# Order of p*v and projection, and the form of the range folds, in the first cross-attention of a Perceiver kernel on Trainium2

## Chip, core and metric

The kernel runs on one core of a Trainium2 chip, in fp32. The metric is the device time of one launch in microseconds (us). Three runs of the kernel before took 1648.14, 1651.96 and 1657.2 us, so the median is 1651.96 us.

## What is computed

128 tokens of 256 features pass through six blocks: a cross-attention to 12544 context rows of 192 features, a causal self-attention, a mixture of eight experts, a second cross-attention, a second self-attention, a second mixture. The change lies in the first block alone:

```python
q = (x @ Wq + bq).reshape(B, N, NUM_HEADS, HEAD_DIM)       # x layer-normed, 16 heads of 16
k = (y @ Wk + bk).reshape(B, M, NUM_HEADS, HEAD_DIM)       # y: the 12544 context rows
v = (y @ Wv + bv).reshape(B, M, NUM_HEADS, HEAD_DIM)
attn = jax.nn.softmax(jnp.einsum('bnhd,bmhd->bhnm', q, k) * scale, axis=-1)
out = jnp.einsum('bhnm,bmhd->bnhd', attn, v).reshape(B, N, IMAGE_DIM)
h = jax.nn.relu(out @ W1 + b1)
return h @ W2 + b2
```

## The kernel before

**Tiling.** The 16 heads are taken as two octets. For each octet the context is walked in 13 superblocks: twelve of 1024 keys, and a short one of 256. A superblock is cut into groups of 256 keys, so an octet has 49 groups and the stage has 98, numbered t = 0 to 97. `groups[t]` is a pair (m, g): superblock and group in it. A group's scores are 2 x 1024 columns on 128 partitions, in two tiles k = 0 and 1.

**Ranges.** The softmax's maximum is not taken over all keys at once. Groups are gathered into ranges of ten, and the fifth range of each octet has nine: ranges b = 0 to 9, where b = 4 and b = 9 are the short ones. A running maximum `mx[b]` is kept during the range. At the range's end `fold(b)` (L442) takes the maximum over the two 256-column halves, `range_maximum` (L455, L456) turns the result on TensorE and reduces it to `negmax`, and one step later (two steps for b = 4) `range_spread` (L255) and `range_spread_out` (L476) write the shift back in the scores' layout, into `spreads[b]`.

**Pipeline.** A step t of the main loop works on several groups at once. TensorE's order is written out by hand:

- `scores(t)` (L411), then `range_spread` where it is due;
- the projection `pieces(t + 4)`: at g = 0 both 64-row parts and the first half of the keys (L214, L217), at g = 1 the second half of the keys, at g = 2 and 3 the same for the values (L232, L239). A short superblock does all four at once;
- `attend(t - 13)`, p*v (L512);
- `range_maximum`, if the range ended with the step before.

`same` in the main loop exchanges projection and p*v: where the superblock that is projected and the one that is attended use the same of the five value tiles (`m % NV`), p*v goes first. For the plain part of the stage that is one step in four, the one with g = 0. In steps 45 to 61, where the short superblock has moved the phase, it is every step.

**The other engines in a step.** ScalarE copies the scores out of PSUM (L424) and takes the exponents of group t - 12 (L499). VectorE takes the running maximum (L430), the fold if one is due, one share of the shift (L488, one SBUF and one PSUM input), and evicts the projections (L372 keys, L376 values, which are queued behind the fold). GpSimd does the larger share of the shift (L488, two SBUF inputs); its instructions for a whole range need only `spreads[b]` and scores kept long ago, so it runs through them without a stop.

**Buffers.** Scores have two PSUM tiles of two banks. Projections and transposes share the two banks of tag "w" (`ps_w`). One bank "m" holds a shift that VectorE still reads. For the two nine-group ranges it is not free when the maximum is due, and both transposes then use "w". A range's probabilities lie in a ring of 28 SBUF tiles (`slot`), which also takes the weights of later blocks. `mx` has one buffer, `spreads` two.

Of the kernel before, what the change touches and what calls it, by code (L numbers as in the profile page):

```python
# [8 lines left out]
F32 = mybir.dt.float32  # L9
AF = mybir.ActivationFunctionType  # L10
ALU = mybir.AluOpType
AX = mybir.AxisListType

P = 128
# [19 lines left out]
def perceiver(ctx: ExitStack, tc: tile.TileContext, a: dict, out: bass.AP):  # L34
    nc = tc.nc
# [17 lines left out]
    def ps_w(name):  # L53
        return banks["pool"].tile([P, KB], F32, tag="w", name=name, bufs=banks["w"])

    def slot(name):

        return ring.tile([P, 2 * KB], F32, tag="p", name=name)
# [32 lines left out]
    ident = const.tile([P, P], F32, name="ident")  # L91
# [97 lines left out]
    NS = (SK + SB - 1) // SB  # L189
# [114 lines left out]
    with tc.tile_pool(name="l0w", bufs=1) as lw:  # L304
# [4 lines left out]
        with psum_pool("ps0", 2) as pp, tc.tile_pool(name="l0x", bufs=1) as work:  # L309
# [3 lines left out]
            AHEAD, LAG = 4, 13  # L313
            NV = 5
            sbs = [(j, s) for j in range(2) for s in range(NS)]
            groups = [(m, g) for m, (j, s) in enumerate(sbs) for g in range(min(SB, SK - s * SB) // 256)]
# [3 lines left out]
            range_of, start_of = [], []  # L320
# [4 lines left out]
            last_of = [t for t in range(len(groups)) if last[t]]  # L325

            kTs, ps, mx, spreads, kept, os, deferred = {}, {}, {}, {}, {}, {}, {}
# [3 lines left out]
            NR = len(start_of)  # L331
# [12 lines left out]
            for j in range(2):  # L344
                pq = ps_mm(f"x0_pq{j}")
                for c in range(2):
                    nc.tensor.matmul(
                        pq[:, :P], xwq[:, c, j * P : (j + 1) * P], xnT[:, c, :], start=(c == 0), stop=(c == 1)
                    )
                qT = work.tile([P, P], F32, tag="qT", name=f"x0_qT{j}", bufs=2)  # L350
                nc.vector.tensor_scalar(
                    qT, pq[:, :P], cols[:, COL_BQ + j : COL_BQ + j + 1], 0.25, ALU.add, ALU.mult
                )
                for u in range(2):
                    nc.vector.tensor_scalar(qz[:, j, u, :], qT, parity[:, u : u + 1], None, ALU.mult)
# [81 lines left out]

            def fold(b):

                for k in (1, 0):  # L440
                    m = mx[b][:, k].rearrange("p a (c n) -> p a c n", c=2)
                    nc.vector.tensor_tensor(m[:, :, 0], m[:, :, 0], m[:, :, 1], ALU.max)  # L442

            def bank_m(name):
                return pp.tile([P, KB], F32, tag="m", name=name, bufs=1)

            def range_maximum(b):
                for k in (1, 0):

                    free = last_of[b] + 1 - LAG + 2 >= start_of[b] - 1  # L450
                    pt = bank_m(f"x0_mt{b}_1") if k and free else ps_w(f"x0_mt{b}_{k}")
                    for a in range(2):
                        for u in range(2):
                            n0 = (2 * a + u) * P
                            nc.tensor.transpose(pt[:, n0 : n0 + P], mx[b][:, k, a, u * P : (u + 1) * P], ident)  # L455
                    nc.vector.tensor_reduce(  # L456
                        negmax[:, b].rearrange("p (u i) -> p i u", u=2)[:, 2 * k : 2 * k + 2],
                        pt.rearrange("p (a u q) -> p a u q", a=2, u=2), AX.X, ALU.max, negate=True,
                    )
# [10 lines left out]
                return pbs  # L470

            def range_spread_out(b, pbs):
                spreads[b] = work.tile([P, 3, 256], F32, tag="spread", name=f"x0_spread{b}", bufs=2)
                for k in range(2):
                    n = 2 - k
                    nc.scalar.copy(spreads[b][:, 2 * k : 2 * k + n], pbs[k][:, :n])  # L476
# [13 lines left out]
            def shifted_gpsimd(t):  # L490
                for k in range(2):
                    shift(nc.gpsimd, t, k, slice(0, shares(t)[k]), spreads[range_of[t]][:, 2 * k :])
# [40 lines left out]
            with tc.manual_schedule():  # L533
                for t in range(AHEAD):
                    for f in pieces(t):
                        f()
                oTs = {}

                spread_at = {max(l + 2, l0 + LAG - 2): b for b, (l0, l) in enumerate(zip(start_of, last_of))}
                for t in range(len(groups) + LAG + 1):  # L540
                    e, o = t - LAG + 1, t - LAG
                    e = e if 0 <= e < len(groups) else None
                    o = o if 0 <= o < len(groups) else None
                    st = scores(t) if t < len(groups) else None
                    ended = range_of[t - 1] if 1 <= t < len(groups) + 1 and last[t - 1] else None
                    b = spread_at.get(t)
                    spread = range_spread(b) if b is not None else None
                    if e is not None:
                        shifted_gpsimd(e)
                        if first[e]:  # L550
                            shifted_vector(e)
                    if t < len(groups):
                        keep(t, st)
                    if spread:
                        range_spread_out(b, spread)
                    if e is not None:
                        for k in range(2):
                            exponent(e, k)
                    if ended is not None:
                        fold(ended)  # L560
                    if 0 <= t - LAG + 2 < len(groups) and not first[t - LAG + 2]:
                        shifted_vector(t - LAG + 2)
                    ahead = pieces(t + AHEAD)

                    same = o is not None and ahead and groups[t + AHEAD][0] % NV == groups[o][0] % NV
                    for f in () if same else ahead:
                        f()
                    if o is not None:
                        attend(o)
                        if last[o]:  # L570
                            oTs[range_of[o]] = collected(range_of[o])
                    for f in ahead if same else ():
                        f()
                    if ended is not None:
                        range_maximum(ended)
                    if t > LAG and last[t - LAG - 1]:
                        g = range_of[t - LAG - 1]
                        gather(g, oTs.pop(g))

                nr = NR // 2  # L580
                acc = work.tile([P, 2, 8, 17], F32, name="x0_acc")
                allneg = small.tile([P, 2, 8], F32, tag="allneg", name="x0_allneg")
                by_octet = negmax.rearrange("p (j b) h -> p j b h", j=2)
                nc.vector.tensor_reduce(allneg, by_octet.rearrange("p j b h -> p j h b"), AX.X, ALU.min)
                fall = work.tile([P, 2, nr, 8], F32, name="x0_fall")
                nc.vector.tensor_tensor(
                    fall, allneg.unsqueeze(2).to_broadcast([P, 2, nr, 8]), by_octet, ALU.subtract
                )
                nc.scalar.activation(fall, fall, AF.Exp)
                nc.vector.tensor_tensor(  # L590
                    accs, accs, fall.rearrange("p j b h -> p (j b) h").unsqueeze(3).to_broadcast([P, NR, 8, 17]),
                    ALU.mult,
                )
                for j in range(2):
                    nc.vector.tensor_reduce(
                        acc[:, j].rearrange("p h d -> p (h d)"),
                        accs[:, j * nr : (j + 1) * nr].rearrange("p b h d -> p (h d) b"), AX.X, ALU.add,
                    )
# [13 lines left out]
            o = slot("x0_o")[:, :D]  # L612
# [23 lines left out]
        with tc.tile_pool(name="l0a", bufs=1) as work:  # L636
# [3 lines left out]
            for j in range(4):  # L640
# [5 lines left out]
                b = cols[:, COL_AQK + j : COL_AQK + j + 1]  # L646
                if j < 2:
                    qT = work.tile([P, P], F32, tag="qT", name=f"a0_qT{j}", bufs=2)
# [11 lines left out]
            acc = work.tile([P, NH, 17], F32, name="a0_acc")  # L660
            for g in range(2):
# [9 lines left out]
                p = work.tile([P, 8, P], F32, tag="ap", name=f"a0_p{g}", bufs=2)  # L671
# [10 lines left out]
            o = normalised(work, acc, 16, "a0_o")  # L682
# [50 lines left out]
    with tc.tile_pool(name="l1x", bufs=1) as work:  # L733
# [6 lines left out]
        ctxs, kTs, vs, ps, mx, sums, spreads, os = {}, {}, {}, {}, {}, {}, {}, {}  # L740
# [4 lines left out]
        qT = work.tile([P, 8, P], F32, name="x1_qT")  # L745
        for g in range(2):
            pq = ps_mm(f"x1_pq{g}")
            for i in range(4):
                j = 4 * g + i
# [185 lines left out]
        with tc.manual_schedule():  # L935
# [7 lines left out]
            for t in range(NP + LAG):  # L943
# [3 lines left out]
                o = attend(before) if 0 <= before else None  # L947
# [4 lines left out]
                k = keys(t + 1) if t + 1 < NP else None  # L952
# [25 lines left out]
                short = k and v and periods[t + 1][1] == NS - 1  # L978
# [180 lines left out]
```

## Time and profile before

| what | value |
|---|---|
| median of three runs | 1651.96 us (1648.14 to 1657.2) |
| the profiled execution's own time | 1656.36 us |
| its span, first to last instruction | 1654.3 us |
| first attention, loop steps 0 to 97 (first scores to the last fold) | 22.0 to 460.7 us |
| GpSimd's first shift of range 0 and of range 8 | 69.50 and 427.51 us |

Busy times are read per engine, and an engine's idle time counts only where it is the one that the others wait for. A line of the timeline gives start, duration, engine, source line, operation, output and inputs with shapes, the number of instructions merged, and in brackets the idle time before it with what ended it. A line of the window table gives, for one stretch, the busy time and instruction count of PE (TensorE's matmuls), PEld (its weight loads), DVE (VectorE), ACT (ScalarE) and POOL (GpSimd), then the share of full clock granted to TensorE and the DMA load.

### The profile page before, as it was taken

The page shows a single profiled execution, that of the slowest core. Times are in us where ns is not written, and L with a number is a line of the kernel's source. Part 1 is how long each engine was busy: PE and PEld are TensorE (multiplying, and loading weights), DVE is VectorE, ACT ScalarE, POOL GpSimd, SP SyncE. Part 2 cuts the span into 40 slices and gives each one's busy share as a digit, 9 for nine tenths or more (in the row PEclk, how much of TensorE's full clock was granted, in tenths as well). Part 3 has the DMA queues.
Part 4 walks back from the last instruction along what each step waited for, and adds up shares of the span by engine and source line. Part 5 has one row for each costly group of instructions (what it writes and reads, how often), then busy time and mean ns, then how long its engine had stood idle before and what let it go on. Part 6 is the DMA issues. An engine that isn't in the chain of part 4 may idle for free.

```text
span 1654.3 us, 39758 instructions
## 1 busy us (share of the span) xinstructions
PE 1540.8 (93%) x17143; PEld 1177.7 (71%) x17143; DVE 1188.2 (72%) x1267; ACT 979.5 (59%) x1178; POOL 857.6 (52%) x554
## 2 busy tenths in 40 slices
PE   7899988999867988999999999999999999999978
PEld 4566655666545874688778777788777777787868
DVE  5788887888874214577777787777777777778952
ACT  2688878889871113466566556566565655665531
POOL 1378777878730000086476575665764864862000
PEclk9999999999986989999999999999999999999979
DMA  3111011111083326423222222332322322234940
GB/s 100 39 59 40 26 59 40 53 46 40 13 272 111 102 52 171 120 79 96 82 78 82 88 87 63 97 90 73 94 78 83 92 82 82 78 97 135 295 141 4
DMA packets 68421, 145.58 MB, mean 88 GB/s; under 512 B 8851, under 2 KB 27027, under 8 KB 68246
## 3 DMA queue, kind: packets, MB, share of 16 engines
q1 hardware_dynamic: 68246, 143.04, 28.9%
q8 instruction: 135, 2.21, 0.6%
q14 instruction: 40, 0.33, 0.1%
HBM read 142.87 MB, written 0.13 MB: 86 GB/s over the span
## 4 chain that ended last, share of the span: by engine, by line
PE 76%; DVE 13%; ACT 8%; issue 2%; DMA 1%; POOLq 0%; ACTq 0%; DVEq 0%; SPq 0%
PE x_k L217 13%; PE x_v L239 11%; PE x_s L808 11%; PE x_o L882 10%; PE x_v L232 6%; PE x_k L214 6%; PE x_s L411 4%; DVE x_mx L430 3%; ACT x_p L424 3%; ACT x_p L499 3%; PE x_o L512 3%; PE f_h L716 2%; PE f_h L1095 2%; PE f_py L726 2%; DVE x_part L905 1%
## 5 line engine op out<-in xcount | busy, mean ns | idle before, releaser
L863 POOL TENSOR_TENSOR x_p<-x_p,x_spread 128x1024 f32<-128x1024 f32 (+1 forms) x175 | 402.8, 2326 | 201.2 <-ACT x_spread L856 201.1
L488 POOL TENSOR_TENSOR x_p<-x_p,x_spread 128x512 f32<-128x512 f32 (+1 forms) x184 | 325.6, 1816 | 142.6 <-ACT x_spread L476 70.1
L905 DVE TENSOR_REDUCE x_part<-x_p 128x256 f32<-128x1024 f32 (+1 forms) x175 | 329.2, 1921 | 1.3 <-ACT x_p L871 1.3
L832 DVE TENSOR_TENSOR x_mx<-x_s,x_mx 128x1024 f32<-128x1024 f32 (+1 forms) x184 | 221.0, 1201 | 148.0 <-PE x_s L808 137.2
L825 ACT COPY x_p<-x_s 128x1024 f32<-128x1024 f32 (+1 forms) x200 | 199.2, 996 | 187.4 <-DVE x_mx L832 108.7
L910 POOL TENSOR_TENSOR x_sums<-x_sums,x_part 128x256 f32<-128x256 f32 x161 | 121.1, 752 | 303.2 <-DVE x_part L905 303.0
L424 ACT COPY x_p<-x_s 128x1024 f32<-128x1024 f32 x196 | 193.4, 1015 | 93.2 <-PE x_s L411 78.6
L239 PEld LDWEIGHTS x_v<-ywv_lo,x_ctx_lo 128*128 128x128 f32 x1568 | 189.3, 192 | 38.3 <-issue 36.8
L808 PE MATMUL x_s<-x_qT,x_kT 64*128 64x128 f32 x3136 | 203.0, 279 | 3.9 <-ACT x_p L825 3.9
L808 PEld LDWEIGHTS x_s<-x_qT,x_kT 64*128 64x128 f32 x3136 | 183.1, 188 | 28.2 <-issue 15.6
L871 ACT ACTIVATE x_p<-x_p 128x1024 f32<-128x1024 f32 (+1 forms) x200 | 197.8, 1037 | 1.4 <-DVE x_p L863 1.3
L499 ACT ACTIVATE x_p<-x_p 128x1024 f32<-128x1024 f32 x196 | 196.3, 1062 | 0.4 <-DVE x_p L488 0.4
L217 PE MATMUL x_k<-x_ctx_lo,ywk_lo 128*128 128x512 f32 (+1 forms) x412 | 194.2, 594 | 0.0
L882 PE MATMUL x_o<-x_p,x_v 128*64 128x128 f32 x3136 | 193.6, 276 | 0.4
L239 PE MATMUL x_v<-ywv_lo,x_ctx_lo 128*128 128x128 f32 x1568 | 193.1, 276 | 0.0
L430 DVE TENSOR_TENSOR x_mx<-x_s,x_mx 128x1024 f32<-128x1024 f32 x140 | 168.1, 1221 | 31.6 <-PE x_s L411 16.8
L882 PEld LDWEIGHTS x_o<-x_p,x_v 128*64 128x64 f32 x3136 | 169.6, 137 | 12.3 <-issue 1.5
L793 ACT COPY x_v<-x_v 128x512 f32<-128x512 f32 (+1 forms) x208 | 116.4, 562 | 76.4 <-PE x_v L239 75.7
L232 PEld LDWEIGHTS x_v<-ywv_hi,x_ctx_hi 64*128 64x128 f32 x1568 | 107.3, 189 | 49.3 <-issue 25.0
L779 ACT COPY x_kT<-x_k 128x512 f32<-128x512 f32 (+1 forms) x104 | 58.3, 561 | 138.2 <-PE x_k L217 138.2
L512 PE MATMUL x_o<-x_p,x_v 128*32 128x128 f32 x3136 | 122.0, 279 | 18.9 <-ACT x_p L499 18.0
L411 PE MATMUL x_s<-x_qz,x_kT 32*128 32x256 f32 x1568 | 119.0, 403 | 15.9 <-ACT x_p L424 15.6
(242 smaller groups left out, 1729.8 us busy)
## 6 DMA issues: line engine op xcount, KB each, us to landing
x_ctx_lo<-in_ctxT_dram SPq DMA_DIRECT2D x131, 512.0 KB, 4.1
x_ctx_hi<-in_ctxT_dram SPq DMA_DIRECT2D x262, 128.0 KB, 4.0
f_w<-in_L_ffn_W_dram SPq DMA_DIRECT2D x32, 512.0 KB, 6.6
f_gating<-n_kernel_gating_EDF_dram SPq DMA_DIRECT2D x8, 512.0 KB, 7.0
f_up<-L_ffn_kernel_up_EDF_dram SPq DMA_DIRECT2D x8, 512.0 KB, 7.3
f_wd<-ffn_kernel_down_EFD_dram SPq DMA_DIRECT2D x8, 512.0 KB, 7.0
x_ctx_lo<-in_ctxT_dram SPq DMA_DIRECT2D x11, 128.0 KB, 2.1
xw<-in_L_xattn_W_dram SPq DMA_DIRECT2D x2, 512.0 KB, 4.8
```

Of the source, the lines that this page charges most:

```text
L217: nc.tensor.matmul(ps[r][:, :h], wk[0][:, js], lo[:, r * h : (r + 1) * h], start=False, stop=True)
L232: nc.tensor.matmul(ps[r][:, ks], hi[rs, ks], wv[1][rs, js], start=(kc == 0), stop=False, skip_group_check=True,)
L239: nc.tensor.matmul(ps[r][:, kc * P : (kc + 1) * P], lo[:, r * h + kc * P : r * h + (kc + 1) * P], wv[0][:, js], start=False, stop=True, sk ...
L424: nc.scalar.copy(ps[t][k], st[k].rearrange("p a n -> p (a n)"))
L430: nc.vector.tensor_tensor(m, st[1 - k], old, ALU.max)
L488: engine.tensor_tensor(v, v, by[:, banks].unsqueeze(2).to_broadcast([P, n, 2, 256]), ALU.add)
L499: nc.scalar.activation(ps[t][k], ps[t][k], AF.Exp)
L808: nc.tensor.matmul(st[:, u, c * P : (c + 1) * P], kTs[t][rs, ks], qT[rs, j, :], start=True, stop=True)
L832: nc.vector.tensor_tensor(mx[j][:, :, : n * P], sts[i], old, ALU.max)
L863: engine.tensor_tensor(v, v, spreads[j].unsqueeze(2).to_broadcast([P, 2, n, P]), ALU.add)
L882: nc.tensor.matmul(o[us, 0:P], vs[t][:, c0 + c, us], p[:, n0 : n0 + P], start=(c0 + c == 0), stop=(c0 + c == total - 1), skip_group_check= ...
L905: nc.vector.tensor_reduce(part, v, AX.X, ALU.add)
```

## The change

1. `same`, the condition under which p*v goes ahead of the projection, is narrowed from "same value tile" to "same tile, and the projection writes the part that p*v reads". It now holds at t = 44, 48, 52, 56, 60 and 93 and no longer at the 27 other steps of 33 (16, 20, ..., 40; 45 to 47; 49 to 51; 53 to 55; 57 to 59; 61, 65, ..., 89).
2. `fold` writes into the tile `spreads[b]` instead of in place, for all ranges. For b = 4 and 9 it is a `tensor_reduce` over pairs (one input) instead of a `tensor_tensor` (two inputs). The transposes of `range_maximum` read `spreads[b]`.
3. `spreads[b]` becomes 4 x 256 instead of 3 x 256 and is taken at the fold. To make room, `qT` has one buffer instead of two, and `x0_acc` and `x0_fall` move into the ring.

```diff
             def fold(b):
+                spreads[b] = work.tile([P, 4, 256], F32, tag="spread", name=f"x0_spread{b}", bufs=2)
                 for k in (1, 0):
-                    m = mx[b][:, k].rearrange("p a (c n) -> p a c n", c=2)
-                    nc.vector.tensor_tensor(m[:, :, 0], m[:, :, 0], m[:, :, 1], ALU.max)
+                    dst, m = spreads[b][:, 2 * k : 2 * k + 2], mx[b][:, k].rearrange("p a (c n) -> p a c n", c=2)
+                    if last_of[b] - start_of[b] < 9:
+                        nc.vector.tensor_reduce(dst, m.rearrange("p a c n -> p a n c"), AX.X, ALU.max)
+                    else:
+                        nc.vector.tensor_tensor(dst, m[:, :, 0], m[:, :, 1], ALU.max)
...
-                            nc.tensor.transpose(pt[:, n0 : n0 + P], mx[b][:, k, a, u * P : (u + 1) * P], ident)
+                            nc.tensor.transpose(pt[:, n0 : n0 + P], spreads[b][:, 2 * k + a, u * P : (u + 1) * P], ident)
...
-                spreads[b] = work.tile([P, 3, 256], F32, tag="spread", name=f"x0_spread{b}", bufs=2)
...
-                    same = o is not None and ahead and groups[t + AHEAD][0] % NV == groups[o][0] % NV
+                    same = False
+                    if o is not None and ahead:
+                        (m, g), (mo, go) = groups[t + AHEAD], groups[o]
+                        short = sbs[m][1] == NS - 1
+                        same = m % NV == mo % NV and (short or g == 3 or (g == 2 and go < 2))
...
-                acc = work.tile([P, 2, 8, 17], F32, name="x0_acc")
+                acc = slot("x0_acc")[:, : 16 * 17].rearrange("p (j h d) -> p j h d", j=2, d=17)
...
-                fall = work.tile([P, 2, nr, 8], F32, name="x0_fall")
+                fall = slot("x0_fall")[:, : 8 * NR].rearrange("p (j b h) -> p j b h", j=2, h=8)
```

## The prediction

> **What bounds the kernel now.** I read the window table first, one stretch per step of a plain superblock (steps 25 to 28, g = 1, 2, 3, 0):
>
> ```profile
> core 0: us, PE busy (x) PEld busy (x) DVE busy (x) ACT busy (x) POOL busy (x), PEclk, DMA share, GB/s
> 126.64:130.26 3.62, 3.21 (x51) 1.83 (x51) 3.13 (x4) 2.63 (x4) 3.62 (x4) 1.00 0.00 0
> 130.26:134.73 4.47, 4.47 (x72) 3.70 (x73) 4.14 (x5) 4.47 (x5) 4.47 (x3) 1.00 0.01 4
> 134.73:138.35 3.62, 3.25 (x61) 2.50 (x57) 3.11 (x5) 3.18 (x5) 3.62 (x3) 1.00 0.15 20
> 138.35:143.36 5.01, 4.62 (x54) 2.30 (x55) 4.21 (x5) 5.01 (x6) 5.01 (x4) 1.00 0.40 142
> ```
>
> TensorE and ScalarE are both nearly full; no engine has room for waits of the other. The last step, where p*v goes first, is the longest, though it has the work of the second (keys for values). TensorE's timeline of it:
>
> ```profile
> 138.35 1.16 PE L411 MATMUL x_s<-x_qz,x_kT 32*128 32x256 f32 x16 [0.37 <-ACT x_p L424]
> 139.44 0.41 PE L512 MATMUL x_o<-x_p,x_v 128*32 128x128 f32 x4
> 140.25 1.07 PE L512 MATMUL x_o<-x_p,x_v 128*32 128x128 f32 x28 [0.39 <-ACT x_p L499]
> 141.25 1.13 PE L214 MATMUL x_k<-x_ctx_hi,xwk_hi 64*128 64x512 f32 x4
> 142.30 1.13 PE L217 MATMUL x_k<-x_ctx_lo,xwk_lo 128*128 128x512 f32 x2
> ```
>
> p*v waits for exponents only just finished. The projection that could have filled the wait follows, and ScalarE then waits for scores(29).
>
> Third, the window table from GpSimd's first shift of one range to that of the next (first row range 1, last row range 4), and the timelines of GpSimd, VectorE and TensorE about the end of range 4:
>
> ```profile
> 113.56:156.66 43.10, 40.96 (x614) 28.72 (x618) 38.04 (x45) 38.93 (x43) 35.75 (x20) 1.00 0.14 40
> 156.66:201.21 44.55, 41.32 (x590) 26.76 (x592) 37.81 (x45) 39.01 (x43) 35.73 (x20) 1.00 0.14 41
> 201.21:251.64 50.43, 44.01 (x598) 29.29 (x594) 40.68 (x47) 39.08 (x43) 35.72 (x21) 0.93 0.16 48
> 251.64:295.37 43.73, 39.34 (x560) 26.78 (x560) 33.53 (x40) 35.36 (x39) 32.14 (x19) 1.00 0.13 38
> ```
>
> ```profile
> 201.21 35.72 POOL L488 TENSOR_TENSOR x_p<-x_p,x_spread 128x1024 f32<-128x1024 f32 x20 [8.81 <-issue]
> ```
>
> ```profile
> 233.07 5.01 DVE L442 TENSOR_TENSOR x_mx<-x_mx 128x512 f32<-128x512 f32 x2
> 238.01 0.68 DVE L488 TENSOR_TENSOR x_p<-x_p,x_m 128x512 f32<-128x512 f32 x1
> 238.61 0.74 DVE L372 TENSOR_SCALAR x_kT<-x_k,cols 128x512 f32<-128x512 f32 x1
> ```
>
> ```profile
> 239.40 0.66 PE L455 MATMUL x_mt<-ident,x_mx 128*128 128x128 f32 x4 [2.34 <-DVE x_kT L372]
> 240.84 1.12 PE L455 MATMUL x_mt<-ident,x_mx 128*128 128x128 f32 x4 [0.79 <-DVE x_negmax L456]
> 241.89 2.09 PE L411 MATMUL x_s<-x_qz,x_kT 32*128 32x256 f32 x16
> ```
>
> The fold's two instructions take 5.01 us; undisturbed (286 us) they take 0.68 each. They end 1.15 us after GpSimd's run ends (201.21 + 35.72 = 236.93; 238.08). Single records agree: the first fold of b = 1, 2, 3, 6, 7, 8 takes 1.35 to 1.78 us, always to about 0.5 us past the end of GpSimd's run; b = 0 and 5, with GpSimd idle, do not. So **a fold cannot end before GpSimd's run plus 1.16 us**. At range 4 TensorE idles 2.34 us behind it and then runs at a clock of 0.53 (step 50, by the window table): scores 2.09 instead of 1.15.
>
> [...] the fold at 233.07 stood through two boundaries between GpSimd instructions. No run here shows a reduce beside a GpSimd stream for this form, but L905 does so in the second attention. [...] about 5.6 us at half rate after 3.1 us of waits within 4 us; the 1.2 us of waits in step 40 cost nothing.
>
> **The change, part by part.**
>
> *Order, plain steps.* With the projection first, a g = 0 step should look like g = 2, as the work is alike. Pair g = 0, 1 now: 5.01 + 3.62 = 8.63; pair g = 2, 3: 4.47 + 3.62 = 8.09. Gain 0.54 per switched step. The exponents are covered by 2.2 us of projection. The context DMAs are issued outside the exchanged part and were requested a superblock earlier; SP's queue is unchanged.
>
> *Order, at range ends and after them.* Steps 20, 40, 69, 89 (6.52 + 3.97) become like 30 and 79 (5.49 + 4.00): up to 1.0 each. Steps 32, 61, 81 (with the next 9.02, or 8.82 at 61) become like 22 and 23 (4.27 + 3.97): 0.6 to 0.8 each.
>
> *What caps it.* Ten-group folds keep two inputs. Faster steps bring them sooner to a GpSimd run that is no shorter: 35.75 + 1.16 (fold's end) + 2.0 (shift 0.6, eviction 0.7, second transposes 0.65) + 4.2 (scores(t + 1), two copies, spread copy) = **43.1 us from run to run**. Two cycles stand there already: 43.10 (above) and 43.05 (339.91 to 382.96), both with the projection first at the range end. So the others fall to 43.1 and no further: 44.06 (0 to 1) gains 1.0, 43.10 nothing, 44.55 gains 1.45, 44.54 (5 to 6) 1.4, 43.05 nothing, 44.55 (7 to 8) 1.45. Sum 5.3 us, where order alone would give 8 to 10. VectorE waits longer at the fold; TensorE then idles about 0.8 us for the transposes, under what cools it.
>
> *Range 3 to 4 (50.43).* The reduce is not in the trace in this form. Nearest rows:
>
> ```profile
> L905 DVE TENSOR_REDUCE x_part<-x_p 128x256 f32<-128x1024 f32 x168 | 324.9, 1973 | 1.3 <-ACT x_p L871 1.3
> L905 DVE TENSOR_REDUCE x_part<-x_p 128x256 f32<-128x512 f32 x7 | 4.8, 680 | 0.0
> ```
>
> The second reduces pairs like the fold: 512 inputs in 0.68, so 1024 in about 1.2[...]. The first reduces fours and is slower, 1.97. I take 1.2, two make 2.4; bounds 2.4 and 3.9[...]. Step 49 now takes 9.91: new, scores end at +1.1, fold at +3.5, shift and eviction +4.8, transposes, negmax 0.7 and transposes again +6.9. Gain 3.0. With waits of 0.4 and 0.75 TensorE stays warm, so step 50 takes 3.62 instead of 5.56: 1.9. Step 47 goes from 5.08 to about 4.5 (0.5, less what step 48 loses as p*v follows p*v). Spread copy 0.2 later against scores. Sum 5.2 us.
>
> *Range 4 to 5 (43.73).* Loss in step 51: its values need the bank that the spread holds until ScalarE's copy. Before, p*v ran meanwhile and 0.52 was idle; now p*v stands behind that wait: 1.0 us lost. Gains: step 53 loses waits of 0.43, 0.40 and 0.84 (1.2); 55 to 58 go from 17.33 to 16.2 (1.1); 59 and 60 from 10.71 to 9.7 (1.0). Sum 2.3. GpSimd's run here is 32.14, so this fold stays free, barely.
>
> *Last range.* No step after 89 is reordered; its fold takes 2.4 instead of 2.6: 0.2.
>
> *Other edits.* The larger spread tile, the separate output, one qT buffer: no instruction more; qT's wait is within VectorE's own order before 22 us. Two ring slots fewer at the end delay each weight DMA by about one step, 2 to 4 us; the first, at 455.87, is needed at 494, and the experts' weights at 543. Nothing, and 3 us if that cover were gone.
>
> *Sum.* 1.0 + 1.45 + 5.2 + 2.3 + 1.4 + 1.45 + 0.2 = 13.0. Span 1654.3 - 13.0 = 1641.3; with the 2.1 us outside it, 1643.4 against 1656.4. The profiled execution lies 4.4 above the median, so 1651.96 - 13.0 = **1639 us**.
>
> **Rivals.**
> A. *The lock does not cap*: what queues behind a late fold has slack. For: at 43.10 TensorE itself had no wait at the fold. Against: evictions and both reductions stand behind it. Gain 13.0 + 5 = 18: 1634.
> B. *The reduce runs at the fours' rate*: 3.9 us, fold at +5.0, TensorE waits 2 us more and cools at range 4 (1.5 + 1.9 lost), and part of the plain gain falls to evictions now on VectorE's path. Gain 8.5: 1643.5.
> C. *Slower: cooling moves to the ten-group folds.* Each fold is met earlier while GpSimd's run is fixed. If TensorE's idle there passes about 2.3 us, as at range 4, where steps 49 to 51 took 21.75 against 15.91 for 59 to 61, each of the six costs 5.8. 35 lost, less 13 gained: +22, 1674. It decides from 2.3 us of idle; I work out 0.8, since a range gains only 1.5 to 3 us on GpSimd's run.
> D. *It does not act*: if p*v is made to wait for the value eviction that now stands before it in the program, steps with g = 2 lose what g = 0 gains; the freed range-4 fold alone remains, about 5: 1647.
>
> **How the numbers follow.** Forecast 0.56, A 0.14, B 0.14, C 0.07, D 0.09. The forecast's own size is uncertain by 4 us (1635 to 1643: the 0.8 us about each fold, run noise of 0.3%). The range 1631 to 1646 takes in A and B, and leaves out C and D. Half a per cent, 8.3 us, is about what a measurement can tell from no change: below 1643.7 is faster. The forecast, A and half of B give 0.77; half of B and D 0.16; C 0.07.
>
> **What would show it.** p*v without waits for L499 in steps 16 to 40; step pairs at 8.1; GpSimd's runs 43.1 apart with the first fold of b = 1, 2, 3, 6, 7, 8 longer than now, 2 to 3.5 us; a reduce of 1.2 us at b = 4; granted clock 1.00 there. I am wrong if runs come under 42.5 apart (A), if the clock falls at ten-group folds (C), or if p*v waits for L376 (D).

## The result and the profile after

The changed kernel takes **1638.52 us** (median of five runs, 1635.42 to 1640.55) against 1652.42 us (five runs of the kernel before). The ratio is 0.9914, with a 95% interval of 0.989 to 0.9938: 13.9 us faster, where 13.0 was forecast.

The profiled execution of after has a span of 1636.7 us, 17.6 less than that of before. The stretch from GpSimd's first shift of range 0 to that of range 8 holds 13.6 us of it (358.0 against 344.4). Most of the rest is not the change's: scores(0) start at 19.77 us instead of 22.00, but at 21.91 in a second profile of the changed kernel; and 1.5 us lie in step 6, where the profile of before shows TensorE at half clock (0.75 over the step) and that of after does not. That is why two single profiles differ by more than the medians.

The window table, one row for each of the plain steps 25 to 28 (g = 1, 2, 3, 0), after:

```profile
121.24:124.86 3.62, 3.21 (x54) 1.83 (x50) 3.09 (x5) 3.09 (x5) 3.62 (x3) 1.00 0.02 5
124.86:129.33 4.47, 4.47 (x72) 3.70 (x72) 4.14 (x5) 4.47 (x5) 4.47 (x4) 1.00 0.00 0
129.33:132.95 3.62, 3.25 (x60) 2.50 (x57) 3.11 (x5) 3.18 (x5) 3.62 (x3) 1.00 0.17 23
132.95:137.30 4.35, 4.35 (x55) 2.30 (x55) 3.97 (x5) 4.35 (x5) 4.35 (x4) 1.00 0.49 166
```

Three rows stand as they were; the last has fallen from 5.01 to 4.35. TensorE's timeline of it:

```profile
132.95 1.16 PE L411 MATMUL x_s<-x_qz,x_kT 32*128 32x256 f32 x16 [0.37 <-ACT x_p L424]
134.04 1.26 PE L214 MATMUL x_k<-x_ctx_hi,xwk_hi 64*128 64x512 f32 x4
135.23 1.12 PE L217 MATMUL x_k<-x_ctx_lo,xwk_lo 128*128 128x512 f32 x2
136.29 1.08 PE L516 MATMUL x_o<-x_p,x_v 128*32 128x128 f32 x32
```

p*v (now L516) runs as one block with no wait: the exponents were finished under the projection. From scores(0) to the end of step 93, waits before p*v fall from 10.5 to 1.4 us.

The window table from GpSimd's run to its next (ranges 1 to 4), after:

```profile
108.62:151.56 42.94, 40.81 (x614) 28.79 (x618) 39.01 (x45) 38.93 (x43) 35.75 (x20) 1.00 0.14 40
151.56:194.56 43.00, 40.74 (x590) 26.76 (x592) 38.94 (x45) 38.87 (x43) 35.77 (x20) 1.00 0.14 42
194.56:239.44 44.88, 39.60 (x566) 26.98 (x562) 37.84 (x47) 38.85 (x43) 35.76 (x21) 1.00 0.18 54
239.44:281.20 41.76, 39.69 (x592) 27.95 (x592) 33.33 (x40) 35.33 (x39) 32.16 (x19) 1.00 0.14 40
```

The six ten-group cycles are now 42.90, 42.94, 43.00, 42.99, 42.95 and 43.02 us, although they had ranged from 43.05 to 44.55. Work that speeds up by different amounts and ends at one number is held by something else. It shows at the end of range 3. VectorE's line for the fold before the change, then the timelines of VectorE and of TensorE after it:

```profile
191.60 1.95 DVE L442 TENSOR_TENSOR x_mx<-x_mx 128x512 f32<-128x512 f32 x2
```

```profile
185.07 3.41 DVE L447 TENSOR_TENSOR x_spread<-x_mx 128x512 f32<-128x512 f32 x2
188.40 0.67 DVE L492 TENSOR_TENSOR x_p<-x_p,x_m 128x512 f32<-128x512 f32 x1
189.00 0.74 DVE L372 TENSOR_SCALAR x_kT<-x_k,cols 128x512 f32<-128x512 f32 x1
```

```profile
189.13 1.32 PE L460 MATMUL x_mt<-ident,x_spread 128*128 128x128 f32 x8 [0.73 <-DVE x_p L492]
```

The fold starts 2.3 us before GpSimd's run ends (151.56 + 35.77 = 187.33) and ends 1.15 us after it, as before; it is simply met sooner (3.41 us instead of 1.95). At range 4, where the fold has one input, VectorE and TensorE show:

```profile
225.82 2.38 DVE L445 TENSOR_REDUCE x_spread<-x_mx 128x512 f32<-128x1024 f32 x2
```

```profile
229.51 0.66 PE L460 MATMUL x_mt<-ident,x_spread 128*128 128x128 f32 x4 [0.37 <-DVE x_kT L372]
230.95 0.66 PE L460 MATMUL x_mt<-ident,x_spread 128*128 128x128 f32 x4 [0.79 <-DVE x_negmax L461]
231.54 1.15 PE L411 MATMUL x_s<-x_qz,x_kT 32*128 32x256 f32 x16
```

GpSimd was busy until 230.3 us, and the reduce took no notice of it: its two instructions took 1.23 and 1.24 us, as the one at 442.35 us did with GpSimd idle (1.23). The wait of 2.34 us and the scores of 2.09 us are gone. VectorE's running maximum (L430) is a `tensor_tensor` too, but with one input in PSUM. Its instructions of one SBUF and one PSUM input take 1.21 to 1.23 us, all 158 of them, the 138 beside an instruction of GpSimd and the 20 others alike. So it is not the operation as such that is held.

### The profile page after: what moved, and what is told of

Its sections match the earlier page's. It is cut to its first block, busy times and chain, and to the rows that moved or that the text cites. A ratio compares the mean times of both kernels' runs of the same rounds, so it can differ in the third digit from the quotient of the medians.

```text
span 1636.7 us, 39760 instructions
## 1 busy us (share of the span) xinstructions
PE 1526.5 (93%) x17143; PEld 1171.0 (72%) x17143; DVE 1191.4 (73%) x1267; ACT 978.6 (60%) x1178; POOL 854.9 (52%) x554
## 4 chain that ended last, share of the span: by engine, by line
PE 75%; DVE 14%; ACT 6%; issue 3%; DMA 1%; SPq 0%; ACTq 0%; DVEq 0%
PE x_k L217 12%; PE x_v L239 12%; PE x_s L816 11%; PE x_o L890 10%; PE x_v L232 6%; PE x_k L214 6%; PE x_s L411 5%; DVE x_mx L430 4%; ACT x_p L424 3%; PE x_o L516 2%; PE f_h L724 2%; PE f_py L734 2%; PE f_h L1103 2%; DVE x_p L492 2%; DVE x_part L913 1%
## 5 line engine op out<-in xcount | busy, mean ns | idle before, releaser
L430 DVE TENSOR_TENSOR x_mx<-x_s,x_mx 128x1024 f32<-128x1024 f32 x140 | 168.0, 1220 | 32.4 <-PE x_s L411 17.6
L516 PE MATMUL x_o<-x_p,x_v 128*32 128x128 f32 x3136 | 112.3, 277 | 9.8 <-ACT x_p L503 9.0
```

What stands on the lines that cost most here:

```text
L430: nc.vector.tensor_tensor(m, st[1 - k], old, ALU.max)
```

## The experiments

My theory: a fold with two SBUF inputs waits for GpSimd's whole run (where it meets one, it ends 1.15 to 1.16 us past the run's end in the profiles of before and after); the new order removes waits, and this lock caps what comes of it; at range 4 the lock was dear. Rivals: step work sets 43.0, or the stall at range 4 has another cause. Each kernel below is the changed one with the edit shown; "cycle" is the time from one run of GpSimd to the next.

**The order alone.**

```diff
-                    if last_of[b] - start_of[b] < 9:
+                    if False:
```

> The changed kernel with every fold by the two-input operation again; the new order of p*v stays. Theory (a two-input fold waits for GpSimd's whole run, and the long wait cools TensorE): ten-group cycles stay at 43.0 us, range 3 to 4 goes from 44.9 back to about 50 us (fold ends 3.3 us later, then some 2 us at half clock), so about 5.5 us slower than the changed kernel, 8 us faster than before, ratio 0.995. Rival (the stall at range 4 comes from both transposes sharing one PSUM bank, or from the order that was changed): range 3 to 4 stays under 46 us and the time within 1 us of the changed kernel, ratio 0.9915.

Measured: 1643.72 us, ratio 0.9948 (0.9929 to 0.9967). Ten-group cycles 42.9 to 43.0; range 3 to 4 back at 49.5. Its fold and the transposes behind it, in the timelines of VectorE and of TensorE:

```profile
227.65 5.61 DVE L447 TENSOR_TENSOR x_spread<-x_mx 128x512 f32<-128x512 f32 x2
```

```profile
234.57 0.66 PE L460 MATMUL x_mt<-ident,x_spread 128*128 128x128 f32 x4 [3.59 <-DVE x_kT L372]
236.01 1.12 PE L460 MATMUL x_mt<-ident,x_spread 128*128 128x128 f32 x4 [0.79 <-DVE x_negmax L461]
```

Steps 50 and 51 run at clocks of 0.78 and 0.81; that of step 51 has a cause of its own, to which I come below. The rival falls: bank and order are those of the changed kernel, and only the fold's form differs.

**The folds alone.**

```diff
-                        same = m % NV == mo % NV and (short or g == 3 or (g == 2 and go < 2))
+                        same = m % NV == mo % NV
```

> The changed kernel with the old order of p*v; the nine-group folds stay one-input. Theory (the parts add): range 3 to 4 falls from 50.4 to about 45.5 us, all other ranges stay at 44.1, 43.1, 44.6, 43.7, 44.5, 43.1, 44.6; about 5 us faster than before, ratio 0.997. Rival (the fold matters only once the order is changed): no difference from before, ratio 1.000.

Measured: 1648.26 us, ratio 0.9974 (0.9964 to 0.9984). The untouched ranges have their old cycles to 0.02 us. Range 3 to 4 fell to 47.7, not 45.5: in the old order the projection still comes behind p*v, so TensorE waits 0.84 us for its eviction and 0.79 for the first reduction, and the next step runs at a clock of 0.64. I had taken 2.3 us of idle as the point where TensorE cools (drops to half clock); that was too high. Alone, the two parts gain 8.7 and 4.2 us, together 13.9; the medians do not tell 12.9 from 13.9.

**All folds by the one-input operation.**

```diff
-                    if last_of[b] - start_of[b] < 9:
+                    if True:
```

> The changed kernel with all ten folds by the one-input operation. Theory (the lock alone holds ten-group cycles at 43.0): folds of b = 1, 2, 3, 6, 7, 8 take 2.5 us instead of 3.0 to 3.5 and no longer end with GpSimd's run, cycles fall to 41.9 to 42.3, about 0.9 us each; b = 0 and 5, never locked, lose up to 1.2 us each; 3 to 5 us faster than the changed kernel, ratio 0.989. Rival (TensorE and ScalarE would need 43.0 anyway): cycles stay at 42.9 to 43.1, the time 0 to 2 us over the changed kernel, ratio 0.9915 to 0.993.

Measured: 1634.48 us, ratio 0.9885 (0.9859 to 0.991), 4 us below the changed kernel's first median. The cycle of range 2 and the fold at its end, in the window table and VectorE's timeline:

```profile
152.93:194.91 41.98, 40.46 (x590) 26.77 (x592) 37.85 (x45) 38.89 (x43) 35.79 (x20) 1.00 0.14 43
```

```profile
186.44 2.38 DVE L445 TENSOR_REDUCE x_spread<-x_mx 128x512 f32<-128x1024 f32 x2
```

Same run of GpSimd, same order, only the second input is gone, and all six cycles are 41.9 to 42.2. Step by step, steps 16 to 94 of the two profiles agree within 0.02 us, except for step 51 and the one behind it, and for the six steps with a ten-group fold beside GpSimd's run: 20, 30, 40, 69, 79 and 89 take 6.03 to 6.53 us with two inputs and 5.37 to 5.50 with one. So 43.0 was the lock, and 42.0 is what the steps take without it. The folds of b = 0 and 5, which I expected to lose, lost nothing: their steps 10 and 59 stay at 6.74 and 5.49. In this profile step 51 took 8.6 us instead of 7.4, at a clock of 0.85; more on that below.

**The same folds with the old order.** The edits of the last two together.

> All ten folds one-input, but the old order of p*v. Theory (with the old, slower steps a ten-group fold came only as GpSimd's run ended, so its lock cost next to nothing): ten-group cycles as before, 43.1 to 44.6 us, and the time within 2 us of the kernel with the old order and one-input folds at nine groups alone, ratio 0.997. Rival (the lock cost something in every order): each of the six cycles shorter by 0.5 us or more, ratio 0.995 or less.

Measured: 1648.17 us, ratio 0.9977 (0.9967 to 0.9987), against 1648.26; every cycle within 0.02 us of the folds alone. With the old order the lock of the ten-group folds cost nothing: the cap came only with the faster steps.

**A shorter and a longer run of GpSimd.** The ten-group folds stay two-input; the share of a range's last group is moved.

```diff
 def shares(t):
...
+                if last[t]:
+                    return 2, 0
```

> The changed kernel, with GpSimd's smaller share of the last group of each range (one instruction of 1.28 us) given to VectorE, whose own instruction for it grows from 0.68 to 1.21 us. Theory (cycle = GpSimd's run + 7.2 us): run 34.5 instead of 35.75, ten-group cycles fall from 43.0 to 41.9 to 42.2, the step work then being the bound; the range 3 to 4 and 4 to 5 cycles stay within 0.5; about 5 us faster than the changed kernel, ratio 0.9885. Rival (the cycle is set by step work and not by GpSimd's run): cycles stay at 43.0 or grow by VectorE's 0.5 us, ratio 0.9915 to 0.994.

```diff
 def shares(t):
...
+                if last[t] and t + LAG - 1 < len(groups):
+                    return 2, 2
...
 def range_spread_out(b, pbs):
...
-                    n = 2 - k
+                    n = 2
```

> The changed kernel, with GpSimd taking the whole shift of the last group of each range; VectorE's 0.68 us for it goes, and ScalarE's second spread copy grows from 0.39 to 0.59 us. Theory (cycle = GpSimd's run + 7.2 us): run 36.8 instead of 35.75, ten-group cycles 44.1 instead of 43.0, some 6 us slower than the changed kernel, ratio 0.995. Rival (GpSimd's run has slack): cycles stay at 43.0 to 43.2 and the time within 1.5 us of the changed kernel, ratio 0.9915.

Measured: shorter 1636.54 us, ratio 0.9904 (0.9889 to 0.992); longer 1643.78 us, ratio 0.995 (0.9931 to 0.9968). The cycle of range 2 in the window table, first of the shorter, then of the longer:

```profile
153.29:195.57 42.28, 40.74 (x590) 26.76 (x592) 38.21 (x45) 38.88 (x43) 34.51 (x20) 1.00 0.14 43
```

```profile
154.48:197.96 43.48, 40.91 (x590) 26.82 (x592) 39.12 (x44) 39.10 (x43) 36.84 (x20) 1.00 0.14 42
```

The cycle follows the run both ways, but not one to one, as I had expected it to: ten-group cycles are 42.2 to 42.3 and 43.4 to 43.5 us, where the forecasts were 41.9 to 42.2 and 44.1. The group whose share I moved is the one whose VectorE shift stands right behind the fold. Moving it changes the 7.2 us too: +0.53 in the shorter (0.68 to 1.21), -0.6 in the longer (the shift is gone). With that, which I worked out only afterwards, run + 7.2 gives 34.51 + 7.73 = 42.24 and 36.84 + 6.6 = 43.44; measured 42.28 and 43.48. The shorter run comes down nearly to the 42.0 that the steps take by themselves, so the longer one says more about the lock. The longer run costs 3.1 us over the eight cycles by the profile, and 5.3 by the medians (6 were forecast); the shorter gains 2.3 and 2.0 (5 were forecast), and its profile has a step 51 at a clock of 0.82.

**Step 51**, where I had forecast a loss. First on top of the one-input folds, then alone.

```diff
-                        same = m % NV == mo % NV and (short or g == 3 or (g == 2 and go < 2))
+                        same = m % NV == mo % NV and (short or g == 3 or (g == 2 and (go < 2 or b is not None)))
```

> The kernel with all folds one-input and, in step 51 alone, p*v ahead of the projection again. Theory (in step 51 the values wait for the bank that the spread holds, and p*v stood behind them for nothing): step 51 falls from 7.4 to 6.3 us, 1 us less than with all folds one-input alone, ratio 0.988. Rival (the saved wait comes back in step 52 as a wait of p*v for exponents): steps 51 and 52 together stay at 11.0 us.

Measured: 1630.56 us, ratio 0.9866 (0.9844 to 0.9889); step 51 takes 6.38, step 52 3.68, so the rival falls. The median is 3.9 us lower than with all folds one-input alone, where 1 was forecast. The profiles account for 2.5 of it: the range 4 to 5 takes 40.81 us instead of 43.32, since step 51 is both shorter and not at half clock. The rest is within what medians of four and six runs leave open.

> The changed kernel with p*v ahead of the projection in step 51 alone. Theory (there p*v only stood behind values that wait for the spread's bank): step 51 at 6.3 to 6.4 us instead of 7.4, all other steps the same, 1.1 us faster than the changed kernel, or up to 2.5 where that wait had also cooled TensorE: ratio 0.9899 to 0.9907. Rival (the wait returns in step 52): steps 51 and 52 together at 11.0, ratio 0.9914.

Measured: 1636.09 us, ratio 0.9905 (0.9884 to 0.9927); steps 51 and 52 take 6.38 and 3.68 against 7.38 and 3.62, so 0.94 us is kept. The median lies 3.3 us below that of the changed kernel measured beside it (1639.41, below), but the runs of the two overlap (1633.97 to 1641.08 and 1635.8 to 1642.69).

> The changed kernel as it is, beside the others on one chip. If the half clock in step 51, seen with the order alone, with all folds one-input and with the shorter GpSimd run but not with the changed kernel, belongs to single executions and not to those kernels, step 51 may be 7.4 or 8.6 us here; otherwise 7.4 again. Ratio 0.9914 either way, within 0.0015.

Measured: 1639.41 us, ratio 0.992 (0.9899 to 0.9941). Step 51 of the changed kernel's first profile, and of this one:

```profile
235.16:242.54 7.38, 5.83 (x80) 4.70 (x80) 4.62 (x7) 6.32 (x8) 3.10 (x2) 1.00 0.00 1
```

```profile
237.31:246.18 8.87, 7.32 (x81) 5.81 (x81) 5.00 (x7) 6.32 (x8) 4.59 (x3) 0.82 0.00 1
```

The same program, with the same wait of 1.55 us in it, cools in one execution and not in the other. So the 8.6 us with all folds one-input were no property of that kernel.

The traces also show what the two executions differ in. Before 460 us, every stretch at half clock, in all twelve profiles, lasts 3.41 us or twice that, and those of one execution start whole multiples of 3.413 us apart. With the order alone they start at 58.16, 235.65, 245.89 and 450.69 us: 52, 3 and 60 times 3.413. The stretches of one execution thus fit one grid of windows of 3.413 us. The window table by this grid, for the second profile (half clock from 242.95) and then for the first (half clock from 429.69, and the grid counted back from there):

```profile
239.54:242.95 3.41, 1.86 (x20) 1.55 (x20) 1.49 (x2) 3.41 (x6) 1.36 (x1) 1.00 0.00 0
242.95:246.36 3.41, 3.41 (x44) 2.71 (x46) 1.28 (x2) 0.68 (x1) 3.41 (x3) 0.50 0.01 2
```

```profile
235.13:238.54 3.41, 2.65 (x26) 1.96 (x26) 3.12 (x5) 3.41 (x4) 0.00 (x0) 1.00 0.00 0
238.54:241.95 3.41, 2.59 (x38) 2.35 (x42) 0.93 (x2) 2.94 (x5) 2.51 (x2) 1.00 0.01 2
```

In the second profile the whole wait lies in one window, TensorE is busy for 1.86 us of it, and the next window runs at half clock. In the first the wait is split over two windows (0.73 and 0.82 us), and the clock stays. Six profiles have this wait, of 1.55 us or (with the shorter run) 1.94: the four where it lies wholly in one window cool, the two where it is split do not. This is read from the traces afterwards; no run moved the wait against the grid on purpose.

With p*v first in that step, the wait is 0.55 us, and none of the three profiles shows the step cool.

> All folds one-input and p*v first in step 51, once more, beside the changed kernel on one chip. Theory: ten-group cycles 42.0, step 51 at 6.4 us, 6 to 8 us faster than the changed kernel in the same call. Rival (its lead of 8 us was partly that chip): 4 us or less.

Measured: 1631.83 us, ratio 0.9874 (0.9851 to 0.9898), 7.6 us below the changed kernel measured beside it, and without overlap of the two (at most 1634.45, at least 1635.8). **All folds one-input with p*v first in step 51** beats both the kernel before and the changed one.

## Why the prediction was right

The terms came true one by one, and not only in their sum. The six ten-group cycles gained 6.05 us (forecast 5.3), range 3 to 4 gained 5.55 (5.2) and range 4 to 5 gained 1.97 (2.3).

*Plain steps.* A switched pair was to fall from 8.63 to 8.09 us; it fell to 7.97 (4.35 + 3.62). The g = 0 step is 0.12 shorter than the g = 2 step it was read from. Right, and slightly under-sized; under the cap the extra 0.12 is worth nothing in ten-group ranges. Steps 32, 61 and 81 with the next fell by 0.75 to 0.76 (forecast 0.6 to 0.8).

*The cap.* Forecast 43.1, measured 42.90 to 43.02. TensorE's idle at the ten-group folds was to be about 0.8 us; the waits are 0.72 to 0.80, with 0.38 at the first. The clock is 1.00 in all eight cycles. The cap can be seen in single steps: 30 and 79, which already had the projection first, grew from 5.49 to 6.46 and 6.53, since they now meet GpSimd's run sooner; 20, 40, 69 and 89 fell only to 6.03 to 6.41. Rival A (no cap) is refuted by these cycles, and the one-input folds, the shorter and the longer run show that the cap is the lock. Rival C (cooling at the ten-group folds) did not happen, but its threshold of 2.3 us of idle, an estimate from the 2.34 us at range 4, was too high: with the folds alone, waits of 0.84 and 0.79 us were followed by a step at a clock of 0.64.

*Range 3 to 4.* Forecast 45.2, measured 44.88: two reduces 2.38 us (forecast 2.4), step 49 6.81 (6.9), step 50 3.62 (3.62), step 47 4.47 (4.5). Step 48 lost nothing, where I had allowed for a little. The row of pairs was the right one to read from; rival B, from the row of fours, is refuted.

*Range 4 to 5.* Forecast 2.3 us, measured 2.0 in the first profile. Step 51 lost 1.1 (forecast 1.0) and steps 55 to 60 gained 2.3 (2.1). The mis-sized term is step 53: 0.6 instead of 1.2. Of its three waits, which add up to 1.67 and not to 1.2, only the 0.40 before p*v went; the one before the scores fell from 0.43 to 0.37, and the one before the transposes of the last range's result from 0.84 to 0.57. What I did not see is that step 51's wait is long enough to cool TensorE in some executions, for some 1.55 us more over steps 51 and 52.

*Last range.* Forecast 0.2 us gained, measured 0.2 lost, from range 8's start to the end of the stage's reduction of maxima (59.56 against 59.37). But in this profile steps 95 and 96 run at clocks of 0.72 and 0.85 and take 0.48 us longer than in the second one, which has 59.21, a gain of 0.16; the forecast stands as far as profiles tell. From there to the last instruction 1167.0 us stand against 1167.4. That shows no cost of the ring slots and the later weights, but only to within some us: in the second profile of the changed kernel the same stretch takes 1161.8. Rival D (a false wait of p*v for the eviction) left no trace: the 1.4 us of waits before p*v are all for exponents.

*The reduce beside GpSimd.* That it would not wait was an estimate, from L905 in the second attention: in the profile of before, its reduces of 1024 inputs take 1.96 to 2.03 us where GpSimd is busy throughout, and 1.94 to 1.95 where it is idle. It held: 1.21 to 1.26 us for every fold by reduce, with GpSimd streaming or not.

*Half clock at range 4.* The stretch, which the prediction put at about 5.6 us, runs from 240.24 to 247.06 in the profile of before, twice 3.41.

## What to carry to other kernels

When several stretches of unequal work end at nearly one period, look for what is queued with fixed length beside them: here a GpSimd stream whose end a two-input VectorE instruction had to await (to 0.55 us past it). Before you speed up the steps around such a meeting point, ask what the partner's end will then cost, and see whether the instruction can be written so that it has one input and need not wait (here 2.38 us for two instructions, against 5.01). In a hand-written order, put work that needs no fresh result in front of work that does, except where the former itself waits for a buffer.

## What the runs showed of the hardware

- The fold with two SBUF inputs, beside a GpSimd stream that never pauses, waited for the stream and not for one instruction of it: its first instruction took 4.42 us at range 4 before and 5.0 us with the order alone, past two boundaries between GpSimd instructions, and in every case to 0.55 us past the stream's end. With GpSimd idle it took 0.68 us.
- Reducing pairs that lie 256 elements apart took as long as the running maximum over as many elements, 1.23 us for 1024 against 1.22; reducing fours in the second attention took 1.97 us. Why, no run here shows.
- TensorE's stretches at half clock start whole multiples of 3.413 us apart within an execution, on a grid that differs from one execution to the next, and the same wait of 1.55 us in step 51 was followed by half clock in one execution of the changed kernel (0.82 over the step) and not in another (1.00). From 90 to 440 us of the twelve profiles, half clock begins after each of the 13 windows with TensorE busy for 1.87 us or less, and after none with 1.95 us or more. Before 90 us it begins after some windows with 2.04 to 2.61 us too, so busy time is not the whole measure; what else counts is open.
- A stretch of 3.41 us at half clock cost 1.5 to 1.6 us in steps 51 and 52 together, against a profile without it. Others fall on step 2, 6, 10 or 14 and cost 1.4 to 1.6 us there, so single profiles of one kernel differ by that much at several places.
